# Norm sums on GpSimd, block transposes on VectorE, and column-tiled products in a four-image convolution network

## Chip, cores and metric

The kernel runs on one core of one Trainium2 chip. The metric is the device time of one execution in microseconds (us). Before the change its median over three runs is 3120.36 us (3120.36 to 3121.54).

## What is computed

Four images of 32 x 32 pixels and 16 channels go through four residual layers. Each layer adds to `x` a function of the group-normed `x` (8 groups of two channels, over all pixels of one image):

```python
x = x + conv(_gn(x), M0, W0, G0)
x = x + conv(_gn(x), M1, W1, G1)
x = x + interval(_gn(x), W0, b0, W1, b1, W2, b2)
x = x + conv(_gn(x), M3, W3, G3)
```

A convolution layer is heavy, because every one of the 1024 output pixels has a 3 x 3 kernel of its own (`G`), which is slid over the whole image:

```python
first   = einsum('ijyx,byxc->bijc', M, inputs)
shifted = conv(inputs, kern)          # 1024 x 16 filters, 3 x 3 x 16
diff    = relu(inputs - shifted)
second  = einsum('ijyx,bijyxc->bijc', W, diff)
return first - second
```

The interval layer pools over intervals (running maximum and minimum of a 32 x 32 triangle) and then does two steps of a dynamic program, with `sigmoid(f @ Wf + r @ Wr + b)` and a maximum over the split point, and a last product with `W2`. `f` is 33 x 33 x 32 for the first step; in the second step, and in the last product, the 16 hidden channels of the step before are put in front of it.

## The kernel before

The four images are two groups of two (`NG`, `GB`). A group's activations are one tile `X[g]`: 128 partitions are 128 pixels, and the free axis holds eight pixel blocks (`NT`) of two images by 16 channels (`GC` = 32). Six phases follow each other, (layer, group) in the order L59 (`phases`) gives; the interval layer is no phase of its own but is done ahead of the last convolution of each group.

**The convolution loop** (`conv_layer`, L457) has 8 pixel blocks x 16 filters x 2 images = 256 tiles in a phase, 1536 in all. A tile is six matmuls (L484): three slots of 64 rows, each as two row halves that run side by side, into a pair of PSUM banks. Slots 0 and 1 are fp32, for which the trace has two records to a matmul, slot 2 is fp32r with one record, so a tile has ten PE records. Then one VectorE instruction (L494) takes the minimum with zero, multiplies by the row of `W` and sums. There are three such bank pairs (`psum`, L55 and L58), and two more single banks (`bank`, L61) for everything else.

**Weights** come in units of eight filters, 16 tiles each: 1.5 MB `raw` by DMA from the SyncE queue, four buffers deep; `prep` (L134) subtracts a mask on GpSimd and starts the third slot on ScalarE, `prep_rest` (L149) finishes it on VectorE.

**The order of the work** is written out by hand, and each engine takes its instructions in program order. What must happen for the next phase is a generator, `behind` (L510). The loop asks it for its next piece after a tile; `yield n` puts the next piece n tiles later (L503 to L505). The pieces for the next phase are `interval_layer` (only ahead of the last convolution layer), `before_conv` and `first_term`. The first `before_conv` runs ahead of the loop, with nothing to hide it (L530 to L537).

**Pieces that matter here.** `group_norm` (L162) sums over the free axis on VectorE (L167), sums over the partitions with a matmul by a matrix of constants (L174), subtracts the mean (L184), does the same with the squares, takes the root on ScalarE (L192) and scales (L195). `before_conv` (L200) then transposes the result with TensorE (L209), copies it from PSUM on ScalarE (L215), writes it to a padded image `xs` in DRAM (L221) and reads it back as shifted copies `im` (L234). `interval_layer` (L325) puts the normed values and their negatives through TensorE transposes (L341), pools with VectorE maxima (L361, L366), and has two steps with GpSimd additions (L417) and VectorE maxima (L424). The left-hand products of a step are in `left` (L379): the output has 128 partitions, four quarters of the rows of `f` by 32 channels. Each quarter is one matmul over the full 128 output columns with a weight that is zero outside its 32 columns, so that four matmuls add up to the tile:

```python
for q in range(NQ):
    nc.tensor.matmul(
        o, lhsT=wf[q], rhs=r[:, QI * q : QI * (q + 1), :],
        start=hidden is None and q == 0, stop=q == NQ - 1,
    )
```

Steps after the first have one more matmul ahead, of the hidden channels by a block-diagonal 128 x 128 weight (L384).

Of the kernel before, what the change touches and what calls it, by code (L numbers as in the profile page):

```python
# [1 line left out]

# [5 lines left out]

F32 = mybir.dt.float32
F32R = mybir.dt.float32r  # L10
AF = mybir.ActivationFunctionType
ALU = mybir.AluOpType
AX = mybir.AxisListType

P = 128
B, H, C = 4, 32, 16
NG = 2
GB = B // NG
GC = GB * C
NL = 3  # L20
NP = H * H
NT = NP // P
HP = H + 2
NPP = HP * HP
HI = H // 2
PITCH = HI * HP
RUN = (HI - 1) * HP + H
ROWS = P // H
# [4 lines left out]
NQ = 4  # L33
QI = H // NQ
# [3 lines left out]
def net_kernel(ctx: ExitStack, tc: tile.TileContext, x, convs, iv_w, iv_b, out):  # L38
# [9 lines left out]
    nc = tc.nc  # L48
    ctx.enter_context(tc.manual_schedule())

    const = ctx.enter_context(tc.tile_pool(name="const", bufs=1))
    wpool = ctx.enter_context(tc.tile_pool(name="wpool", bufs=2))
    work = ctx.enter_context(tc.tile_pool(name="work", bufs=1))
# [7 lines left out]
    def bank(name):  # L61
        return psum.tile([P, 512], F32, tag="one", bufs=2, name=name)
# [24 lines left out]
    load_chunk(0)  # L87


    mean_w = const.tile([P, P], F32, name="mean_w")  # L90
    nc.vector.memset(mean_w, 1.0 / (2 * NP))
    eps = const.tile([P, 1], F32, name="eps")
    nc.vector.memset(eps, 1e-5)
    ident = const.tile([P, P], F32, name="ident")
# [22 lines left out]

    xs = [dram.tile([GC, NPP], F32, name=f"xs{g}") for g in range(NG)]
    zero = const.tile([P, HP], F32, name="zero")
    xt = [const.tile([P, 2, ROWS, HP], F32, name=f"xt{g}") for g in range(NG)]  # L120
    im = [const.tile([P, 3, GB, PITCH], F32, name=f"im{g}") for g in range(NG)]
    im9 = [const.tile([P, GB, PITCH], F32R, name=f"im9{g}") for g in range(NG)]

# [35 lines left out]
    def pair_view(ap):  # L159
        return ap.rearrange("p t (g s) -> p t g s", s=2)  # L160

    def group_norm(g, name, dst):  # L162


        def sums(src, name):
            part = work.tile([P, GC // 2], F32, tag="part", name=f"part_{name}")
            nc.vector.tensor_reduce(  # L167
                part, src.rearrange("p t (g s) -> p g t s", s=2), axis=AX.XY, op=ALU.add
            )
            return part  # L170

        def mean_of(part, name):
            ps = bank(f"ps_{name}")
            nc.tensor.matmul(ps[:, : GC // 2], lhsT=mean_w, rhs=part, start=True, stop=True)  # L174
            return ps[:, : GC // 2]

        part = sums(X[g], f"m{name}")
        yield 2
        m = mean_of(part, f"m{name}")
        yield 1  # L180
        mean = work.tile([P, GC // 2], F32, tag="mean", name=f"mean_{name}")
        nc.vector.tensor_copy(mean, m)
        xc = work.tile([P, NT, GC], F32, tag="xc", name=f"xc_{name}")
        nc.vector.tensor_tensor(pair_view(xc), pair_view(X[g]), spread(mean), ALU.subtract)  # L184
        yield 1
        sq = work.tile([P, NT, GC], F32, tag="sq", name=f"sq_{name}")
        nc.vector.tensor_tensor(sq, xc, xc, ALU.mult)
        part = sums(sq, f"v{name}")
        yield 2
        v = mean_of(part, f"v{name}")  # L190
        rstd = work.tile([P, GC // 2], F32, tag="rstd", name=f"rstd_{name}")
        nc.scalar.activation(rstd, v, AF.Sqrt, bias=eps)  # L192
        yield 2
        nc.vector.reciprocal(rstd, rstd)
        nc.vector.tensor_tensor(pair_view(dst), pair_view(xc), spread(rstd), ALU.mult)  # L195
        yield 2

    xns = {}

    def before_conv(g, layer):  # L200
        xn = work.tile([P, NT, GC], F32, tag="xn", bufs=2, name=f"xn_{g}_{layer}")
        xns[g] = xn
        yield from group_norm(g, f"c{g}{layer}", xn)

        ps = bank(f"ps_t{g}{layer}")
        for m in range(2):
            nc.tensor.transpose(  # L209
                ps[:, m * P : (m + 1) * P],  # L210
                xn[:, 4 * m : 4 * m + 4, :].rearrange("p t m -> p (t m)"),
                ident,
            )
        yield 1
        nc.scalar.copy(  # L215
            xt[g][:, :, :, 1 : 1 + H],
            ps[:, : 2 * P].rearrange("p (m r x) -> p m r x", m=2, x=H),
        )
        inner = xs[g][:, HP : HP + H * HP].rearrange("p (m t n) -> p t m n", m=2, t=4)
        for t in range(4):  # L220
            (nc.scalar if t % 2 else nc.sync).dma_start(  # L221
                inner[:, t],
                xt[g][GC * t : GC * (t + 1)].rearrange("p m r x -> p m (r x)"),
            )
        yield 2
        xsv = xs[g].rearrange("(b c) n -> c b n", b=GB)
        at = 0
        for slot, row, tap in [(2, row, 8) for row in range(4)] + [
            (tap // 4, tap % 4, tap) for tap in range(8)
        ]:  # L230
            for h in range(2):
                off = (HI * h + tap // 3) * HP + tap % 3
                r0 = 64 * h + C * row
                (nc.scalar, nc.sync)[at % 2].dma_start(  # L234
                    im[g][r0 : r0 + C, slot, :, :RUN], xsv[:, :, off : off + RUN]
                )
                at += 1
        yield 9
        halve(im9[g], im[g][:, 2], low_x)
        yield 2  # L240
        halve_rest(im9[g], im[g][:, 2], low_x)
# [37 lines left out]
    def constants():  # L279
        nc.vector.tensor_reduce(  # L280
            stack, ident.rearrange("p (j m) -> p m j", m=GC), axis=AX.X, op=ALU.add
        )
        nc.scalar.dma_start(wv, iv_w)
        nc.scalar.dma_start(bv, iv_b)
        mask8 = const.tile([P, 8], F32, name="mask8")
        nc.vector.tensor_reduce(
            mask8, ident.rearrange("p (k c) -> p k c", c=C), axis=AX.X, op=ALU.add
        )
        mask2 = const.tile([P, GB], F32, name="mask2")
        nc.vector.tensor_reduce(  # L290
            mask2, ident.rearrange("p (s b c) -> p b s c", b=GB, c=C), axis=AX.XY, op=ALU.add
        )
        yield 2

        def blocks(dst, k, mask, n):
            p = dst.shape[0]
            nc.gpsimd.tensor_tensor(
                dst,
                wv[:p, k, :].unsqueeze(1).to_broadcast([p, n, C]),
                mask[:p].unsqueeze(2).to_broadcast([p, n, C]),  # L300
                ALU.mult,
            )

        for k, name in ((0, "f0"), (3, "f1"), (6, "f2")):

            t = const.tile([64, (2 * NQ - 1) * GB, C], F32, name=name)
            nc.gpsimd.memset(t, 0.0)
            at = (NQ - 1) * GB
            blocks(t[:, at : at + GB, :], k, mask2, GB)
            t = t.rearrange("p k c -> p (k c)")  # L310
            iv[name] = [t[:, GC * (NQ - 1 - q) : GC * (NQ - 1 - q) + P] for q in range(NQ)]
            yield 1
        for k, name in ((1, "r0"), (4, "r1")):
            t = const.tile([64, NQ * GB, C], F32, name=name)
            for q in range(NQ):
                blocks(t[:, q * GB : (q + 1) * GB, :], k, mask2, GB)
            iv[name] = t.rearrange("p k c -> p (k c)")
            yield 1
        for k, name in ((2, "h1"), (5, "h2")):
            t = const.tile([P, 8, C], F32, name=name)  # L320
            blocks(t, k, mask8, 8)
            iv[name] = t.rearrange("p k c -> p (k c)")
            yield 1

    def interval_layer(g):  # L325

        R = 2 * GC
        xn2 = ivp.tile([P, NT, 2, GC], F32, tag="xn2", name=f"xn2_{g}")
        yield from group_norm(g, f"i{g}", xn2[:, :, 0, :])
        nc.gpsimd.tensor_scalar_mul(xn2[:, :, 1, :], xn2[:, :, 0, :], -1.0)  # L330

        M = H // 2
        pp = [ivp.tile([R, H + M, M + H], F32, tag=f"pp{k}", name=f"pp{k}_{g}") for k in range(2)]
# [1 line left out]
            nc.gpsimd.memset(t, -BIG)  # L335
        yield 3
        raw = pp[1][:, :H, M:]
        for half in range(2):
            ps = bank(f"ps_iv{g}{half}")
            for t in range(4):  # L340
                nc.tensor.transpose(  # L341
                    ps[:R, t * P : (t + 1) * P],
                    xn2[:, 4 * half + t].rearrange("p s m -> p (s m)"),
                    ident,
                )
            yield 1
            nc.scalar.copy(
                raw[:, HI * half : HI * (half + 1), :],
                ps[:R].rearrange("p (i j) -> p i j", j=H),
            )  # L350
        upper = [[-1, H], [1, H]]
        nc.gpsimd.affine_select(
            out=pp[0][:, :H, M:], in_=raw, pattern=upper, compare_op=ALU.is_ge, fill=-BIG,
# [25 lines left out]
        def left(name, wf, hidden=None, wh=None):  # L379

            ps = bank(f"ps_{name}{g}")
            o = ps[:, : QI * T1]
            if hidden is not None:
                nc.tensor.matmul(o, lhsT=wh, rhs=hidden, start=True, stop=False)  # L384
            for q in range(NQ):
                nc.tensor.matmul(  # L386
                    o, lhsT=wf[q], rhs=r[:, QI * q : QI * (q + 1), :],
                    start=hidden is None and q == 0, stop=q == NQ - 1,
                )
            return o.rearrange("p (i k) -> p i k", k=T1)  # L390

# [135 lines left out]
        if phase == len(phases) - 1:  # L527
            nc.sync.dma_start(out[1 - g], X[1 - g])

    start = before_conv(*phases[0])  # L530
    next(start)
    v = ident.rearrange("p (h q c) -> p q c h", h=2, q=4)
    nc.vector.tensor_reduce(pick, v[:, 0], axis=AX.X, op=ALU.add)
# [72 lines left out]
```

## Time and profile before

| Figure | Value |
|---|---|
| Span of the profiled execution | 3119.8 us |
| VectorE busy | 2100.3 us, 67% |
| ScalarE busy | 147.2 us, 5% |
| GpSimd busy | 289.2 us, 9% |
| Convolution matmuls, slots 0 and 1 (L484) | 12288 records, 2920.4 us |
| VectorE reduction of a tile (L494) | 1536 of 1224 ns |
| Norm sums by matmul (L174) | 4 groups of records, 6.8 us busy together |
| Transposes ahead of a convolution (L209) | 12 of 324 ns |
| Transposes of the interval layer (L341) | 16 of 279 ns |
| Left products (L386 and L384) | 48 records of 391 ns and 8 of 438 ns |
| Granted TensorE clock | 1.000 |

Busy time of a matmul record says little alone, since records overlap: the convolution's two row halves run side by side. The chain of work that ended last, in order of time, is the view to read: it follows the span back from its last instruction, and each piece begins where the one before it ends. A piece `PE pc L484 x40` is a run of 40 convolution records, that is four tiles.

### The profile page before, as it was taken

How to read it: one execution, taken by the hardware profiler on the slowest of the kernel's cores; microseconds unless marked ns; L12 is line 12 of the kernel's file. 1: busy time of each engine (PE TensorE's matmuls, PEld its weight loads, DVE VectorE, ACT ScalarE, POOL GpSimd, SP SyncE). 2: the span in 40 equal slices, each digit the busy share in tenths (PEclk: the TensorE clock that was granted, in tenths of full speed). 3: DMA queues.
4: the chain of work that ended last, by engine and by line, in shares of the span. 5: the costliest groups of instructions: out<-in, count | busy, mean ns of one | idle time of the engine just before them, and what ended most of it. 6: DMA issues, size and time to landing. Idle time of an engine off the chain costs nothing.

```text
span 3119.8 us, 37923 instructions
## 1 busy us (share of the span) xinstructions
PE 3089.7 (99%) x15792; PEld 1568.0 (50%) x15792; DVE 2100.3 (67%) x3348; ACT 147.2 (5%) x159; POOL 289.2 (9%) x173
## 2 busy tenths in 40 slices
PE   6999999999999999999999999999999999999999
PEld 4444455444444444444446654444664444444444
DVE  4656666666666666666677766667776666666666
ACT  0000000000000000000000000000100000000000
POOL 2000000000000000000013300002230000000000
PEclk9999999999999999999999999999999999999999
DMA  4322111321111231211111132121113211111100
GB/s 144 123 102 75 48 68 48 125 75 66 50 62 60 69 124 48 75 48 68 48 70 52 48 118 75 48 75 48 68 48 103 97 48 70 48 72 51 67 28 2
DMA packets 32462, 215.21 MB, mean 69 GB/s; under 512 B 5665, under 2 KB 7713, under 8 KB 18465
## 3 DMA queue, kind: packets, MB, share of 16 engines
q1 hardware_dynamic: 27168, 207.02, 18.4%
q10 hardware_dynamic: 4992, 5.74, 0.9%
q8 instruction: 124, 2.03, 0.3%
q14 instruction: 50, 0.40, 0.0%
q0 software_dynamic: 128, 0.02, 0.0%
HBM read 211.64 MB, written 1.12 MB: 68 GB/s over the span
## 4 chain that ended last, share of the span: by engine, by line
PE 99%; DMA 1%; DVE 0%; ACTq 0%; issue 0%; ACT 0%
PE pc L484 97%; PE pf L255 1%; PE pfs L263 0%; DMA im<-xs 0%; PE ps_l L386 0%; DMA X<-in_x 0%; PE ps_r L397 0%; PE ps_l L384 0%; PE ps_t L209 0%; PE ps_vc L174 0%; PE ps_iv L341 0%; DMA xs<-xt 0%; PE ps_mc L174 0%; DVE xc_c L184 0%; ACTq L234 0%; DVE junk L494 0%
## 5 line engine op out<-in xcount | busy, mean ns | idle before, releaser
L484 PE MATMUL pc<-im,raw 64*128 64x512 f32 x12288 | 2920.4, 590 | 13.2 <-DMA im<-xs 13.2
L494 DVE SCALAR_TENSOR_TENSOR junk<-pc,WT 128x1024 f32<-128x1024 f32 x1536 | 1880.0, 1224 | 990.4 <-PE pc L484 986.6
L484 PEld LDWEIGHTS pc<-im,raw 64*128 64x128 f32 x12288 | 1237.2, 186 | 1137.5 <-issue 746.6
L484 PE MATMUL pc<-im,W 64*128 64x512 f32 x3072 | 1293.2, 803 | 0.0
L484 PEld LDWEIGHTS pc<-im,W 64*128 64x128 f32 x3072 | 321.1, 186 | 355.6 <-issue 343.5
L140 POOL TENSOR_TENSOR raw<-raw,pick 128x1024 f32<-128x1024 f32 x96 | 182.0, 1898 | 2278.5 <-DMA raw<-in_g 2216.9
L111 ACT ACTIVATE W<-raw,low_w 128x1024 fp32r<-128x1024 f32 x96 | 110.3, 1149 | 2198.0 <-PE pc L484 2170.1
L494 DVE DVE_READ_ACCUMULATOR junk<-pc,WT 128x1 f32 x1536 | 127.6, 83 | 0.0
L114 DVE SCALAR_TENSOR_TENSOR W<-raw,low_w,W 128x1024 fp32r<-128x1024 f32 x96 | 122.9, 1280 | 0.0
L417 POOL TENSOR_TENSOR dp_b<-ft_b,rt_r 128x1089 f32<-128x1089 f32 x16 | 39.1, 2449 | 101.6 <-ACT ft_b L410 51.5
L417 POOL TENSOR_TENSOR dp_a<-ft_a,rt_r 128x1089 f32<-128x1089 f32 x16 | 37.2, 2327 | 79.9 <-DVE s_a L424 50.2
L255 PE MATMUL pf<-MT,xn 128*32 128x512 f32 x192 | 23.1, 598 | 0.0
L424 DVE TENSOR_REDUCE s_b<-dp_b 128x33 f32<-128x1089 f32 x16 | 20.5, 1283 | 0.0
L424 DVE TENSOR_REDUCE s_a<-dp_a 128x33 f32<-128x1089 f32 x16 | 20.5, 1282 | 0.0
L114 DVE SCALAR_TENSOR_TENSOR im<-im,low_x,im 128x1088 fp32r<-128x1088 f32 x6 | 9.1, 1523 | 14.6 <-DMA im<-xs 14.6
L259 ACT COPY fs<-pf 128x512 f32<-128x512 f32 x12 | 7.0, 586 | 240.1 <-PE pf L255 240.1
L330 POOL TENSOR_SCALAR xn<-xn 128x256 f32<-128x256 f32 x2 | 1.7, 856 | 151.0 <-DVE xn L195 151.0
L506 DVE TENSOR_TENSOR X<-X,acc 128x32 f32<-128x32 f32 x48 | 13.6, 283 | 1.6
L263 PEld LDWEIGHTS pfs<-stack,fs 128*128 128x128 f32 x96 | 11.2, 191 | 3.4 <-issue 3.4
L361 DVE TENSOR_TENSOR pp<-pp 64x1024 f32<-64x1024 f32 x10 | 12.1, 1213 | 0.0
L366 DVE TENSOR_TENSOR pp<-pp 64x1024 f32<-64x1024 f32 x10 | 12.1, 1213 | 0.0
L255 PEld LDWEIGHTS pf<-MT,xn 128*32 128x32 f32 x192 | 5.0, 109 | 14.1 <-issue 14.1
(81 smaller groups left out, 160.1 us busy)
## 6 DMA issues: line engine op xcount, KB each, us to landing
raw<-in_g SPq DMA_DIRECT2D x96, 1536.0 KB, 6.6
WT<-in_w SPq DMA_DIRECT2D x48, 512.0 KB, 6.3
MT<-in_mt SPq DMA_DIRECT2D x12, 2048.0 KB, 8.3
im<-xs SPq DMA_DIRECT2D x72, 67.8 KB, 3.2
im<-xs ACTq DMA_DIRECT2D x72, 67.8 KB, 3.3
xs<-xt SPq DMA_DIRECT2D x12, 34.0 KB, 1.7
xs<-xt ACTq DMA_DIRECT2D x12, 34.0 KB, 1.8
X<-in_x ACTq DMA_DIRECT2D x2, 128.0 KB, 5.1
```

Source lines behind the costliest of these rows:

```text
L111: nc.scalar.activation(dst, src, AF.Copy, scale=mask[:, 1:2])
L114: nc.vector.scalar_tensor_tensor(dst, src, mask[:, 0:1], dst.bitcast(F32), op0=ALU.mult, op1=ALU.add)
L140: nc.gpsimd.tensor_tensor(raw[:, 1], raw[:, 1], pick[:, f0 : f0 + FU].unsqueeze(2).to_broadcast([P, FU, P]), ALU.subtract,)
L255: nc.tensor.matmul(ps[32 * j : 32 * j + 32, :], lhsT=xn[:, pt, :], rhs=mt[:, pt, :], start=pt < 4, stop=pt >= 4, tile_position=(0, 32 * j),)
L263: nc.tensor.matmul(ps[:, GC * t : GC * (t + 1)], lhsT=fs[:, t // 4, t % 4 * P : (t % 4 + 1) * P], rhs=stack, start=True, stop=True,)
L361: nc.vector.tensor_tensor(pp[k][:, :H, M:], a[:, :H, M:], a[:, s : H + s, M:], ALU.max)
L366: nc.vector.tensor_tensor(pp[k][:, :H, M:], a[:, :H, M:], a[:, :H, M - s : M - s + H], ALU.max)
L417: nc.gpsimd.tensor_tensor(t, ft[:, i, :].unsqueeze(1).to_broadcast([P, T1, T1]), rt, ALU.add,)
L424: nc.vector.tensor_reduce(s[:, i - 1, :], last, axis=AX.X, op=ALU.max)
L484: nc.tensor.matmul(ps[:, h, :], lhsT=w[:, f % FU, :], rhs=v[:, :, :H], start=slot == 0, stop=slot == 2,)
L494: nc.vector.scalar_tensor_tensor(junk, ps.rearrange("p h n -> p (h n)"), 0.0, chunks[n], op0=ALU.min, op1=ALU.mult, accum_out=acc[:, t, co ...
L506: nc.vector.tensor_tensor(X[g][:, t], X[g][:, t], acc[:, t], ALU.add)
```

## The change

It takes work off TensorE.

- **Norm sums.** The sum over partitions becomes GpSimd's `partition_all_reduce` on the 128 x 16 partial sums. The division by the number of elements moves into the multiplication that copies the mean, and into the scale of the root. The waits are rewritten: five tiles lie between the sum and its use instead of one for the mean, and five more for the variance. The first norm, ahead of the loop, keeps the matmul (`on_pe=True`).
- **Transposes.** VectorE's `transpose`, which transposes blocks of 32 x 32, replaces TensorE's transposes and the copies from PSUM. Ahead of a convolution it is one instruction over 128 x 256; in the interval layer it is four over 32 x 256, and the negatives are then made by one ScalarE multiplication. As the layout of a block transpose differs, the store to `xs` is in runs of one image row (34 numbers) instead of four rows.
- **Left products.** A quarter has a 32-column weight and writes only its own 32 output partitions; the hidden product is four 32 x 32 products on the diagonal in place of one of 128 x 128.
- The constants shrink with it (`f0` to `f2`, `h1`, `h2`, no `mask8`).

```diff
         def mean_of(part, name):
+            if not on_pe:
+                m = work.tile([P, GC // 2], F32, tag="sum", name=f"sum_{name}")
+                nc.gpsimd.partition_all_reduce(m, part, channels=P, reduce_op=bass_isa.ReduceOp.add)
+                return m
             ps = bank(f"ps_{name}")
-            nc.tensor.matmul(ps[:, : GC // 2], lhsT=mean_w, rhs=part, start=True, stop=True)
+            nc.tensor.matmul(ps[:, : GC // 2], lhsT=ones, rhs=part, start=True, stop=True)
             return ps[:, : GC // 2]
 
         part = sums(X[g], f"m{name}")
         yield 2
         m = mean_of(part, f"m{name}")
-        yield 1
+        yield 5
         mean = work.tile([P, GC // 2], F32, tag="mean", name=f"mean_{name}")
-        nc.vector.tensor_copy(mean, m)
+        nc.vector.tensor_scalar_mul(mean, m, 1.0 / (2 * NP))
...
         v = mean_of(part, f"v{name}")
+        yield 5
         rstd = work.tile([P, GC // 2], F32, tag="rstd", name=f"rstd_{name}")
-        nc.scalar.activation(rstd, v, AF.Sqrt, bias=eps)
+        nc.scalar.activation(rstd, v, AF.Sqrt, bias=eps, scale=1.0 / (2 * NP))
...
-        ps = bank(f"ps_t{g}{layer}")
-        for m in range(2):
-            nc.tensor.transpose(
-                ps[:, m * P : (m + 1) * P],
-                xn[:, 4 * m : 4 * m + 4, :].rearrange("p t m -> p (t m)"),
-                ident,
-            )
-        yield 1
-        nc.scalar.copy(
-            xt[g][:, :, :, 1 : 1 + H],
-            ps[:, : 2 * P].rearrange("p (m r x) -> p m r x", m=2, x=H),
-        )
-        inner = xs[g][:, HP : HP + H * HP].rearrange("p (m t n) -> p t m n", m=2, t=4)
-        for t in range(4):
-            (nc.scalar if t % 2 else nc.sync).dma_start(
-                inner[:, t],
-                xt[g][GC * t : GC * (t + 1)].rearrange("p m r x -> p m (r x)"),
-            )
+        nc.vector.transpose(
+            xt[g][:, :, 1 : 1 + H], xn
+        )
+        inner = xs[g][:, HP : HP + H * HP].rearrange("p (t r n) -> p r t n", r=ROWS, n=HP)
+        for r in range(ROWS):
+            (nc.scalar if r % 2 else nc.sync).dma_start(inner[:, r], xt[g][GC * r : GC * (r + 1)])
...
-        for half in range(2):
-            ps = bank(f"ps_iv{g}{half}")
-            for t in range(4):
-                nc.tensor.transpose(
-                    ps[:R, t * P : (t + 1) * P],
-                    xn2[:, 4 * half + t].rearrange("p s m -> p (s m)"),
-                    ident,
-                )
-            yield 1
-            nc.scalar.copy(
-                raw[:, HI * half : HI * (half + 1), :],
-                ps[:R].rearrange("p (i j) -> p i j", j=H),
+        for row in range(ROWS):
+            nc.vector.transpose(
+                raw[:GC].rearrange("p (t r) j -> p r t j", r=ROWS)[:, row], xi[H * row : H * (row + 1)]
             )
+        yield 1
+        nc.scalar.mul(raw[GC:], raw[:GC], -1.0)
...
+            quarters = [slice(GC * q, GC * (q + 1)) for q in range(NQ)]
             if hidden is not None:
-                nc.tensor.matmul(o, lhsT=wh, rhs=hidden, start=True, stop=False)
-            for q in range(NQ):
+                for s in quarters:
+                    nc.tensor.matmul(o[s], lhsT=wh[s], rhs=hidden[s], start=True, stop=False)
+            for q, s in enumerate(quarters):
                 nc.tensor.matmul(
-                    o, lhsT=wf[q], rhs=r[:, QI * q : QI * (q + 1), :],
-                    start=hidden is None and q == 0, stop=q == NQ - 1,
+                    o[s], lhsT=wf, rhs=r[:, QI * q : QI * (q + 1), :],
+                    start=hidden is None, stop=True,
                 )
...
-    start = before_conv(*phases[0])
+    start = before_conv(*phases[0], on_pe=True)
```

## The prediction

> **What bounds the kernel now.** I read the page's busy shares first, then its chain of work that ended last, then stretches of that chain in order of time.
>
> ```profile
> PE 3089.7 (99%) x15792; PEld 1568.0 (50%) x15792; DVE 2100.3 (67%) x3348; ACT 147.2 (5%) x159; POOL 289.2 (9%) x173
> PE 99%; DMA 1%; DVE 0%; ACTq 0%; issue 0%; ACT 0%
> ```
>
> TensorE is 99% of the chain: from the first convolution tile on nothing else ends last. So whatever is taken out of its stream shortens the kernel, and work on other engines costs nothing until it stops that stream. What does one small matmul cost there? The chain from 540 to 660 us (start, length, what), around the norm and transpose for one convolution:
>
> ```profile
> 553.49 0.33 PE ps_mc L174 x2
> 553.81 8.05 PE pc L484 x40
> 561.86 0.32 PE ps_vc L174 x2
> 562.18 8.04 PE pc L484 x40
> 570.23 0.37 PE ps_t L209 x2
> 570.60 51.16 PE pc L484 x256
> 621.75 1.85 PE pf L255 x16
> ```
>
> Runs of 4 and of 26 tiles (x256 has four records missing) took 8.04 and 51.16 us: (51.16 - 8.04) / 22 = 1.960 us a tile. From the mean's matmul to the variance's are 8.37 us, four tiles are 7.84, so one norm sum costs 0.53 us, not its 0.33: the run behind it loses 0.20 as the array empties and refills. The variance's costs 0.53 too; the transposes cost 570.23 to 621.75 less 26 tiles, 51.52 - 50.96 = 0.56. The interval layer of the second group, in the same view:
>
> ```profile
> 2118.68 0.56 PE ps_iv L341 x4
> 2119.24 2.16 PE pc L484 x9
> 2121.40 0.56 PE ps_iv L341 x4
> ...
> 2188.66 1.56 PE ps_l L386 x7
> 2190.22 62.94 PE pc L484 x320
> ...
> 2260.87 0.64 PE ps_l L384 x2
> 2261.51 1.75 PE ps_l L386 x7
> ```
>
> A half of its transposes costs 2.72 - 1.96 = 0.76. The first left product costs 1.56 + 0.20 = 1.76; one with hidden channels 0.64 + 1.75 + 0.20 = 2.59.
>
> Is VectorE near the limit? A tile takes 1224 + 83 ns of 1.960 us, 0.65 us is free. There are three bank pairs, so I estimate that it may run 2 x 1.96 - 1.27 = 2.65 us late before TensorE waits. Where two extra operations meet (timeline of VectorE):
>
> ```profile
> 1617.59 1.21 DVE L361 TENSOR_TENSOR pp<-pp 64x1024 f32<-64x1024 f32 x1
> 1618.73 1.27 DVE L114 SCALAR_TENSOR_TENSOR W<-raw,low_w,W 128x1024 fp32r<-128x1024 f32 x1
> 1619.92 1.21 DVE L494 SCALAR_TENSOR_TENSOR junk<-pc,WT 128x1024 f32<-128x1024 f32 x1
> ```
>
> The tile's reduction before began at 1616.44, so this one is 1.5 us late, yet the chain there is one run of 30 tiles in 59.00 us, 30 x 1.960 + 0.20.
>
> **What the Trainium skill says.** "TensorE: Matmul & The Clock Gate", Part 3 (Packing small matmuls): tiles in different column groups run at once, for little more than the time of one. The trace agrees: `pf` is 8 matmuls of 512 columns on four column tiles (L255), 16 records; in sequence they would need 16 x 0.43 = 6.8 us (the first left product, 8 passes of 264 columns in 1.76, gives 0.22 a pass, and so 0.43 for 512), and they cost 1.85 + 0.20 = 2.05. "TensorEngine Tiling (Array Packing)", Key Properties: changing the tiling mode drains the array; its Gotcha 1 says that different row tiles cannot use one PSUM bank at the same time. The drain is seen: `ps_l` without hidden channels, on 64 rows as the convolution, costs what its passes cost, while the 128-row hidden matmul adds 0.83 for two passes, 0.44, so about 0.39 for a mode and back; `pf` gives 2.05 - 4 x 0.43 = 0.33. The bank rule no trace here shows. "GPSIMD Engine Reference", section 3.2, has a partition-axis reduction of 128 x 2048 at 247.7 us; section 2.1 puts a first call to a freshly loaded kernel near 6 us. No run here shows either.
>
> **The change, part by part.**
>
> *Norm sums.* On PE, two leave each of five convolution norms and two interval norms (the first norm keeps its matmuls): 14 x 0.53 = -7.4 us. GpSimd gets 14 reductions of 16 columns. The skill's rate gives 247.7 / 2048 x 16 = 1.9 us; with 6 for a load, about 8 (estimates). Low bound: one small GpSimd operation, 0.23 us (L297). High bound: I allow 20. I take 2 to 8. The wait this adds: VectorE's multiplication for the mean stands 2 + 5 tiles, 13.7 us, behind the partial sum, and behind it queue the tile reductions, for whose bank pairs TensorE waits. The variance has 9 tiles, 17.6 us, to VectorE's reciprocal, with ScalarE's root between, behind which only weight preparation queues. So up to 13 us cost nothing. On GpSimd, mask subtractions queue behind the sum, but they run about two units ahead (2216.9 us of its idling is for a unit's DMA), and before, it sat 75.6 us for the interval norm (L330) without TensorE noticing. Cost 0.
>
> *Transposes.* On PE -5 x 0.56 - 4 x 0.76 = -5.8 us. VectorE gets five of 128 x 256 and eight of 32 x 256. "VectorE: DVE Perf Modes", The three transpose paths, has 128 x 128 at 311 ns in bf16; the nearest row here is a multiplication of 128 x 256, 0.42 us (L187). I take 0.42; upper bound twice that. Interval: four in one go, 1.7 us (3.4 at most), within 2.65 as priced, over it by under 1 us twice at the bound. Cost 0. The ScalarE negation replaces two copies of 0.58, hidden in four tiles.
>
> *Left products.* The first: two rounds of four tiles, 2 x 0.22 + 0.33 for the mode = 0.77, saves 1.0, twice: -2.0. With hidden channels, if the four diagonal tiles overlap: 4 x 0.22 for both products, and three mode changes at about 0.18, 0.55: 1.43, saves 1.16, four times: -4.6. If the one shared bank makes the diagonal tiles wait for each other, 8 passes in place of 2 add 1.3 each: +5.3 in all.
>
> *Start.* Ahead of the loop nothing hides. Out go transposes and copy, 13.56 to 14.86 in the chain, 1.30 us; in comes one transpose with its handover, 0.5: -0.8. The store to `xs` has 1024 pieces of 136 B for 256 of 544 B. Its stretch was 2.10 us; pieces of 544 B took 32 ns. At 32 again, 64 a DMA engine instead of 16, it grows by 48 x 0.032 = 1.5; at 17 (what the 4-byte ones beside them take) by 0.6; at three times 32, as "DMA: Bandwidth & Descriptors" (table at its head) warns of read-modify-write under 512 B, by 5.6. I take +1.2: net +0.4. Later stores lie under nine tiles of waiting: cost 0. The longer waits make the interval phase some 191 of 256 tiles long, so nothing runs over its end.
>
> Sum: -7.4 - 5.8 - 2.0 - 4.6 + 0.4 = -19.4; 3120.4 - 19.4 = 3101.
>
> **Rivals.**
> A, all hides and the tiles overlap: 3101. Chance 0.62.
> B, the diagonal tiles run one after another, or modes cost double: 3101 + 5.3 = 3106. For: the bank rule. Against: `pf` overlaps in one bank, though with one row group. 0.16.
> C, the pieces of 136 B cost 96 ns at the start, and the block transposes take twice as long and stop TensorE: 3101 + 4.4 + 2 = 3107. 0.10.
> D, slower: GpSimd's sum is the new bound. At 20 us it is 6.3 beyond the mean's 13.7, of which 2.65 are absorbed: 3.7 x 7 = 26 us; the variance exceeds its 17.6 by 2.4, absorbed: 3101 + 26 = 3127. At 25 us: 8.7 + 4.8 = 13.5 x 7 = 94, 3195. For: GpSimd operations are the slowest here (2449 ns at L417), and nothing shows this one. Against: 16 columns are little. 0.08.
> E, a sum of 17 to 20 us eats the gain, or other stops do: 3114 to 3126. 0.04.
>
> **How the numbers follow.** A's time is predicted. The range takes A to C with their unknowns: 3097 (store without growth, cheaper modes) to 3112; D, E and 0.05 of tails lie outside. Faster by over 0.2% means under 3114.1: A, B, C, 0.88. Same is E, 0.04, slower D, 0.08.
>
> **What would show it.** In the chain after, `ps_mc`, `ps_vc`, `ps_t`, `ps_iv` are gone after the first tile, and convolution runs pass there at 1.960 a tile. `ps_l` pieces with 0.20 added give 0.77 and 1.43; 2.7 with hidden channels is B. GpSimd's sum under 13 us, and VectorE's wait for it zero; a wait of VectorE for it, followed by TensorE waiting for `junk`, is D. First steady tile at 29.89 + 0.4. Wrong it would be by a sum over 13.7 us, or by transposes near 1 us each.

## The result, and the profile after

The changed kernel takes 3103.43 us (median of six runs, 3102.53 to 3106.23), the kernel before 3120.57 (3119.03 to 3121.54). The ratio is 0.9947, 95% interval 0.9934 to 0.9960: 17 us faster, where 19.4 were forecast. In the pair of profiled executions the span falls from 3119.8 to 3100.8 us.

The page's busy shares and the engines of the chain that ended last, after the change:

```profile
PE 3069.8 (99%) x15760; PEld 1506.1 (49%) x15760; DVE 2114.4 (68%) x3361; ACT 145.7 (5%) x151; POOL 294.3 (9%) x182
PE 99%; DMA 1%; DVE 0%; issue 0%; ACTq 0%; ACT 0%; DVEq 0%
```

TensorE is the bound as before. The stretch of the chain that answers to the norm and transpose of one convolution (start, length, what; the view begins at 480 us, in the midst of a run):

```profile
479.65 151.71 PE pc L463 x774
631.36 1.85 PE pf L248 x16
```

Where the kernel before had three interruptions ahead of the first term, there is one run of convolution tiles. And the left products of the second group's interval layer, in the same view:

```profile
2189.68 0.58 PE ps_l L365 x8
2190.26 62.97 PE pc L463 x320
...
2260.93 0.58 PE ps_l L363 x8
2261.51 0.58 PE ps_l L365 x8
```

A run of tiles takes 0.20 us beyond its tiles, called refilling below. With it, the first product costs 0.78 us (1.76 before), one with hidden channels 1.36 (2.59 before). GpSimd's timeline around an interval norm, with the idle time ahead of an operation and its releaser in brackets:

```profile
1563.59 0.45 POOL L175 PARTITION_ALL_REDUCE sum_mi<-part_mi  x1 [58.19 <-DVE part_mi L167]
1580.70 0.44 POOL L175 PARTITION_ALL_REDUCE sum_vi<-part_vi  x1 [16.67 <-DVE part_vi L167]
1588.59 1.89 POOL L140 TENSOR_TENSOR raw<-raw,pick 128x1024 f32<-128x1024 f32 x1 [7.44 <-issue]
```

A sum takes 0.45 us and starts when VectorE hands it the partial sums. The next weight preparation comes 7.44 us behind the sum, in which GpSimd waited for nothing that the profile shows. Such a pause of 7.1 to 7.5 us lies between a sum and the next weight preparation throughout. The expectations below call it a load; the profile gives it no name.

Two things are there that the forecast did not have. One is a stop of TensorE at the first group's interval layer. Timeline of VectorE around it:

```profile
1606.19 1.77 DVE L323 STREAM_TRANSPOSE pp<-xi 32x256 f32<-32x256 f32 x4
...
1609.14 4.27 DVE L114 SCALAR_TENSOR_TENSOR W<-raw,low_w,W 128x1024 fp32r<-128x1024 f32 x1
```

And of GpSimd:

```profile
1609.19 1.27 POOL L329 TENSOR_SCALAR_AFFINE_SELECT pp<-pp 64x1024 f32<-64x1024 f32 x1 [14.80 <-ACT pp L327]
1610.44 1.89 POOL L140 TENSOR_TENSOR raw<-raw,pick 128x1024 f32<-128x1024 f32 x1
```

VectorE's weight operation (L114) takes 4.27 us instead of 1.28, while two GpSimd operations run; it ends 1.08 us behind the second of them. It stands behind the burst of four transposes, so the reductions are late, and TensorE waits: from 1177.16 us the chain takes 488.72 us for 248 tiles, and in the second profile of the same kernel, without the stop, 486.69. So one tile takes 2.03 us more than the others.

The other is in the tile itself. A long uninterrupted run in the chain after, and one before:

```profile
668.75 471.00 PE pc L463 x2400
```

```profile
1168.72 403.96 PE pc L484 x2055
```

240 tiles in 471.00 - 0.20 us are 1.9617 us each. The 206 tiles before (some records are missing) took 403.96 - 0.20, 1.9600 each. Over 1535 tiles 0.0017 us are 2.6 us, more than the forecast's step for the first left products (2.0).

The start of the loop also differs from execution to execution: VectorE's first reduction began at 32.62 us in the profile before, at 30.49 in the one after, and at 33.52 in a second profile of the changed kernel (e0_after below). The second reduction came 3.13, 1.97 and 3.77 us behind the first, where a tile is 1.96. So the profile after had a start 3.3 us shorter than the one before, by chance, and the 19.0 us between the two spans agree with the forecast's 19.4 better than they should. Differences of some 3 us between single profiles are not read as effects here; medians over runs and lengths of pieces are.

### The profile page after: what moved, and what is told of

It reads as the page before. It is cut to its first block, busy times and chain, and to the rows that moved or that the text cites. A ratio compares the mean times of both kernels' runs of the same rounds, so it can differ in the third digit from the quotient of the medians.

```text
span 3100.8 us, 37902 instructions
## 1 busy us (share of the span) xinstructions
PE 3069.8 (99%) x15760; PEld 1506.1 (49%) x15760; DVE 2114.4 (68%) x3361; ACT 145.7 (5%) x151; POOL 294.3 (9%) x182
## 4 chain that ended last, share of the span: by engine, by line
PE 99%; DMA 1%; DVE 0%; issue 0%; ACTq 0%; ACT 0%; DVEq 0%
PE pc L463 97%; PE pf L248 1%; PE pfs L256 0%; DMA im<-xs 0%; DMA X<-in_x 0%; DVE junk L473 0%; PE ps_r L376 0%; PE ps_l L365 0%; DMA xs<-xt 0%; PE ps_l L363 0%; DVE xc_c L188 0%; DVE pp L323 0%; PE ps_y L427 0%; PE ps_vc L178 0%; DVE xt L212 0%
## 5 line engine op out<-in xcount | busy, mean ns | idle before, releaser
L473 DVE SCALAR_TENSOR_TENSOR junk<-pc,WT 128x1024 f32<-128x1024 f32 x1536 | 1879.7, 1224 | 958.5 <-PE pc L463 953.2
L463 PEld LDWEIGHTS pc<-im,raw 64*128 64x128 f32 x12288 | 1187.5, 186 | 1185.1 <-issue 800.5
L463 PE MATMUL pc<-im,W 64*128 64x512 f32 x3072 | 1251.1, 804 | 0.0
L463 PEld LDWEIGHTS pc<-im,W 64*128 64x128 f32 x3072 | 298.7, 186 | 365.8 <-issue 364.8
L114 DVE SCALAR_TENSOR_TENSOR W<-raw,low_w,W 128x1024 fp32r<-128x1024 f32 x96 | 134.6, 1402 | 0.0
L114 DVE SCALAR_TENSOR_TENSOR im<-im,low_x,im 128x1088 fp32r<-128x1088 f32 x6 | 8.1, 1347 | 13.3 <-DMA im<-xs 13.3
```

Of the source, the lines that this page charges most:

```text
L114: nc.vector.scalar_tensor_tensor(dst, src, mask[:, 0:1], dst.bitcast(F32), op0=ALU.mult, op1=ALU.add)
L463: nc.tensor.matmul(ps[:, h, :], lhsT=w[:, f % FU, :], rhs=v[:, :, :H], start=slot == 0, stop=slot == 2,)
L473: nc.vector.scalar_tensor_tensor(junk, ps.rearrange("p h n -> p (h n)"), 0.0, chunks[n], op0=ALU.min, op1=ALU.mult, accum_out=acc[:, t, co ...
```

## The experiments

**The three parts alone.** Theory: a matmul taken out of the stream is worth its piece in the chain and the 0.2 us of refilling, and the other engines hide what they get. Rival: what GpSimd does about its sums, or VectorE's bursts, disturbs the loop and gives some of it back. Each part of the diff was put into the kernel before by itself. The norm sums:

```diff
+            if not on_pe:
...
+                nc.gpsimd.partition_all_reduce(m, part, channels=P, reduce_op=bass_isa.ReduceOp.add)
...
-            nc.tensor.matmul(ps[:, : GC // 2], lhsT=mean_w, rhs=part, start=True, stop=True)
...
-        yield 1
+        yield 5
```

> Only the norm sums move to GpSimd, with their new waits; transposes and left products stay as before. Price theory (each matmul taken out of the stream is worth its piece plus 0.2 us of refilling, and nothing else changes): 14 x 0.525 = 7.4 us less than before, so near 3113; no wait of TensorE for VectorE; first tile as before, near 29.9 us. Rival (the [...]7.2 to 7.5 us that GpSimd pays after a sum, and the sums themselves, disturb the loop): the steady tile grows from 1.960 to about 1.962 us here and not in the other two parts, which gives back some 2.6 us, so near 3116.

3112.78 us against 3119.88, ratio 0.9976 (0.9967 to 0.9985): 7.1 us, as the pieces say (7.4). A run of 217 tiles in the chain:

```profile
1182.67 425.52 PE pc L489 x2170
```

(425.52 - 0.20) / 217 = 1.9600. GpSimd's sums and pauses do not touch the tile. The transposes:

```diff
-            nc.tensor.transpose(
-                ps[:, m * P : (m + 1) * P],
...
+        nc.vector.transpose(
+            xt[g][:, :, 1 : 1 + H], xn
+        )
```

> Only the transposes move to VectorE, with the store in runs of one image row; sums and left products as before. Price theory: 5 x 0.57 + 4 x 0.755 = 5.9 us less, and if the start of the changed kernel came from this part, 2 us more, so near 3112.5: the reads of the padded image at the start take 88 ns a piece as in the changed kernel, not 215. Rival (the shorter start was chance): the reads take 215 ns again, the start is 0.4 us longer than before, and the time is near 3115. If a burst of four transposes on VectorE stops TensorE by itself, each of the two bursts costs up to 2 us more.

3115.08 us, ratio 0.9984 (0.9977 to 0.9990): 4.8 us, 3.1 to 7.2 by the interval. The pieces are 5.9; the start takes something back. The store to the padded image, in the chain of this kernel:

```profile
14.58 3.45 DMA xs<-xt
```

It ends at 18.03 us, where before it was 15.25 + 2.10 = 17.35: +0.7. The reads behind it took 186 ns a piece of 2168 bytes (median), and in the changed kernel's second profile 216, so the 88 ns of its first profile were chance. There was no stop at either burst of transposes here. The left products:

```diff
-            t = const.tile([64, (2 * NQ - 1) * GB, C], F32, name=name)
...
+            t = const.tile([64, GB, C], F32, name=name)
...
+                for s in quarters:
+                    nc.tensor.matmul(o[s], lhsT=wh[s], rhs=hidden[s], start=True, stop=False)
-            for q in range(NQ):
+            for q, s in enumerate(quarters):
```

> Only the left products go on 32-column tiles. Price theory: the first product falls from 1.78 to 0.78 us and those with hidden channels from 2.615 to 1.353, 2 x 1.0 + 4 x 1.26 = 7.1 us less, so near 3113.5; the steady tile stays at 1.960. Rival (changes of tiling mode or smaller weights change the loop's own rate): the steady tile differs from 1.960 here.

3115.09 us, ratio 0.9985 (0.9978 to 0.9991): 4.8 us and not 7.1, although the products cost what was expected (0.58 us a piece). The tile is why; a run of 206 tiles:

```profile
1169.15 404.30 PE pc L478 x2060
```

(404.30 - 0.20) / 206 = 1.9617: the rival's answer, and in this part alone. And the whole change again, on the same chip as its parts:

> The changed kernel again, on the chip of its parts. If the parts add up: 3120.5 less the three gains. If the steady tile of 1.962 us was chance of chip or run, it is 1.960 here; if it belongs to the program, 1.962 again. The stop of 2.0 us near 1613 us [...]may come or not.

3105.84 us, ratio 0.9956 (0.9942 to 0.9969). The three gains add to 16.7, measured are 14.0 here and 17.1 in the first comparison. The interval here reaches from 9.7 to 18.1 us, so the parts may simply add up; no loss from their meeting is shown. The tile is 1.9617 us again (240 tiles in 471.00), so it belongs to the program. The stop near 1613 us did not come: there VectorE's weight operation took 1.28 us.

**What slows the tile.** The run just quoted ends at 1573 us, and the first left product in that trace is at 1666, so the products themselves do not slow it. But this part also shrinks the constants (`f0` to `f2`, `h1`, `h2`, `mask8`) by 3104 bytes a partition, and the weight buffers lie behind them: `raw` begins at byte 59200 of a partition instead of 62304. An unused constant moves them by 32:

```diff
+        pad = const.tile([P, 8], F32, name="pad")
+        nc.gpsimd.memset(pad, 0.0)
         mask2 = const.tile([P, GB], F32, name="mask2")
```

> The changed kernel with one unused constant of 32 bytes a partition ahead of the buffers that follow the constants, so that the weights lie at 59232 instead of 59200 in a partition; nothing else differs. Address theory (the smaller constants moved the weights from an address that is 32 past a multiple of 64 to a multiple of 64, and this slows every tile by 0.0017 us): the steady tile is 1.960 us again and the time 2.6 us under the changed kernel's. Rival (the column-tiled products themselves, or the shift of some 3 KB, slow the loop): 1.9617 us stays.

> The kernel before with the same unused 32 bytes: the weights move from 62304 to 62336, a multiple of 64. Address theory: the steady tile grows to about 1.9617 us and the time by 2.6 us, near 3122.5. Rival: 1.960 us and 3120 stay.

The changed kernel with the pad: 3101.57 us, ratio 0.9943 (0.9930 to 0.9955). The kernel before with it: 3124.57 us, ratio 1.0015 (1.0008 to 1.0021). One long run of the first and one of the second:

```profile
669.92 470.60 PE pc L465 x2396
```

```profile
1169.05 404.64 PE pc L486 x1864
```

240 tiles (four records missing) in 470.40 are 1.9600 us, 206 tiles in 404.44 are 1.9633. So 32 bytes that nobody reads bring the changed kernel's tile back, and cost the kernel before 4.9 us. (In time alone the pad's gain for the changed kernel is not clear of the noise, since the two intervals overlap; the length of its tile is.) It is the address of what lies behind the constants: the granted clock reads 1.00 in all these runs of tiles, and VectorE's reduction takes 1224 ns on average in every one of the kernels. By the remainder of `raw`'s address on division by 128, the tile took:

| Remainder | Kernels | us a tile |
|---|---|---|
| 96 | before, e1_norms, e2_transposes, f1_after_pad, and the padded h1 and i1 below | 1.9600 |
| 64 | the changed kernel (two profiles), e3_left, g1 below | 1.9617 |
| 0 | f2_before_pad | 1.9633 |
| 32 | j1 and j2 below | 1.960 to 1.967, changing from phase to phase |

j1 and j2 differ in their late sums too, so the last row is no test of the address alone. The images `im`, TensorE's other operand, lie ahead of the constants and stay where they are, but other buffers moved with `raw`. Which of them counts, and whether 128 is the period, stays open.

**Are the long waits needed?** The sums are ready 0.45 us behind the partial sums. The waits were set back:

```diff
         m = mean_of(part, f"m{name}")
-        yield 5
+        yield 1
...
         v = mean_of(part, f"v{name}")
-        yield 5
```

> The changed kernel with the waits of the kernel before: one tile instead of five ahead of the mean's use, none instead of five ahead of the root. If a sum takes the 0.45 us that the record shows[...], VectorE never waits for it and the time is that of the changed kernel within 1 us. Rival (a load of 7.2 to 7.9 us lies between partial sum and sum): where one does, VectorE waits 2 to 4 us for it, and TensorE stops up to 2 us at each, up to some 15 us in all.

3102.41 us (3100.88 to 3102.84), ratio 0.9943 (0.9931 to 0.9956). No time is lost. Timeline of GpSimd at a norm of the first phase, and then of VectorE:

```profile
54.04 0.45 POOL L175 PARTITION_ALL_REDUCE sum_mc<-part_mc  x1 [14.64 <-DVE part_mc L167]
```

```profile
59.38 0.17 DVE L186 TENSOR_SCALAR mean_c<-sum_mc 128x16 f32<-128x16 f32 x1
```

The sum is there at 54.49 and used at 59.38. GpSimd had been idle for 14.64 us when the partial sum came, since its weight preparation runs units ahead, so a pause on the way into the sum is hidden in that time; the one behind the sum keeps nobody waiting.

**The stop behind the burst.** Is it the burst of 1.77 us, or the meeting of VectorE's two-input operation with GpSimd's? The weight operation was moved by two tiles, the burst left alone, in the padded kernel:

```diff
-                if f % FU == 4:
+                if f % FU == 5:
                     prep_rest(u + 1)
```

> The padded changed kernel with the weights' second half (the two-input VectorE operation of 1.28 us) two tiles later in each unit; the interval layer's four transposes stay in one burst. Port theory (the stop of 2.04 us needs that VectorE operation to meet a GpSimd operation, which holds it up to 4.27 us, right behind the burst): no stop at either burst, and a time 0 to 4 us under the padded kernel's 3101.6, depending on how many of its runs were hit. Rival (the burst of 1.77 us alone stops TensorE): a stop of some 2 us stays at one or both bursts.

3099.80 us (3099.47 to 3101.97), ratio 0.9938 (0.9925 to 0.9950). VectorE's timeline at the first burst:

```profile
1606.71 1.77 DVE L325 STREAM_TRANSPOSE pp<-xi 32x256 f32<-32x256 f32 x4
...
1612.59 1.35 DVE L114 SCALAR_TENSOR_TENSOR W<-raw,low_w,W 128x1024 fp32r<-128x1024 f32 x1
```

The burst is as long as before, the weight operation short again, and no tile at either burst is longer than the others. The padded kernel f1_after_pad, which differs in this alone, had a stop of 2.0 us at both bursts in its profile, with L114 at 4.27 us each time. One profile without stops would be weak, since the stop comes and goes, but all profiles agree: of the twelve bursts in after, e0_after, e2_transposes, f1, g1 and i1, the three with L114 at 4.27 us behind them have the stop, the nine others, with 1.35 at most, have none. So the burst alone does no harm; with a weight operation held behind it, it does. In the profile after, weight operations of 3.31 and 3.37 us away from a burst (at 1674.79 and 2190.87) stop nothing; whether 4.27 alone would was not tried. It is a near tie: at the second group's burst, L114 began at 2127.26 and GpSimd's selection at 2127.31, the same 0.05 us apart as at the first, and there VectorE took 1.28 us and the selection 2.37 instead of 1.27. The Trainium skill ("GPSIMD Engine Reference", section 1, Specifications) says that GpSimd's memory interfaces are shared with VectorE and contended by VectorE instructions with two SBUF inputs. The traces agree: L114 reads two SBUF tiles; the tile reduction, which reads PSUM and one SBUF tile, took 1223 ns on average in the 220 cases where a GpSimd two-input operation overlapped it, and 1224 over all.

**What late sums would cost.** The forecast's slower case was never tried by the change itself. A detour makes each sum late without changing its value:

```diff
-                return m
...
+                nc.gpsimd.tensor_tensor(share, m, per_p, ALU.mult)
...
+                nc.gpsimd.partition_all_reduce(again, share, channels=P, reduce_op=bass_isa.ReduceOp.add)
+                return again
```

In j1_late_sums the waits stay long; j2_late_sums_short has those of g1_short_waits as well.

> The padded changed kernel with GpSimd's sums made late on purpose: behind each sum a two-input operation and a second sum,[...] so that the result comes some 16 us behind the partial sum instead of 0.45. The result is the same number. The waits stay at five tiles. By the working of the prediction's slower case, the mean is due after 13.3 us, so VectorE gets it 2.7 us late, of which 2.65 are absorbed, and the variance is due after 17 us: no more than 1 us lost in all, near 3101. Rival (nothing is absorbed): 7 x 2.7 = 19 us lost.

> The same late sums with the waits of the kernel before (one tile ahead of the mean's use, none ahead of the root). The mean is due after 5.5 us and comes 10.5 late, of which 2.65 are absorbed: 7.9 lost; the variance is due after 7.1 us and comes 8.9 late: 6.3 lost; seven norms lose 7 x 14.2 = 99 us, near 3200, and TensorE waits for VectorE's reduction there. If GpSimd hides the loads in another way, the loss is smaller than half of that.

With the long waits 3127.78 us, ratio 1.0028 (1.0018 to 1.0039), where no more than 1 us was expected to be lost: 26 us over the padded kernel. GpSimd's timeline at a norm of the second phase:

```profile
567.92 0.21 POOL L177 TENSOR_TENSOR share_mc<-sum_mc,per_p 128x16 f32<-128x16 f32 x1 [7.46 <-issue]
574.12 0.44 POOL L179 PARTITION_ALL_REDUCE again_mc<-share_mc  x1 [5.99 <-issue]
```

VectorE's there, and at the variance in the first phase:

```profile
98.82 0.25 DVE L203 RECIPROCAL rstd_c<-rstd_c 128x16 f32<-128x16 f32 x1 [12.54 <-ACT rstd_c L201]
...
574.59 0.17 DVE L190 TENSOR_SCALAR mean_c<-again_mc 128x16 f32<-128x16 f32 x1 [1.33 <-POOL again_mc L179]
```

The pauses of 7.46 and 5.99 us come wherever GpSimd goes from a sum to a two-input operation or back, 5.7 to 8.6 us each in j1 and j2. At the second phase's mean VectorE waits 1.33 us and no tile grows: lateness within the slack is absorbed, as worked out. But at 90.9 us one tile takes 11.9 us more: TensorE stands for 9.84 us, and the next 3.67 us it runs at a granted clock of 0.50. There, in the first phase, a weight preparation stood between the two sums and brought two further pauses, so that the variance's sum began 12 us late. At the two interval layers the late sums delay GpSimd's fill of `pp`, the transposes wait for that (2.2 us at the first), and then meet the weight operation: stops of 4.3 and 5.2 us. The tile, at yet another address (remainder 32 in the table), is 1.960 to 1.967 us from phase to phase, 5.6 us in all. 11.9 + 4.3 + 5.2 + 5.6 = 27, against a padded execution without stops.

With short waits 3219.60 us, ratio 1.0319 (1.0305 to 1.0333). Its waits (who, for whom, us in total, times, longest):

```profile
PE pc L470 <- DVE junk L480: 82.5, 14, 8.9
...
DVE mean_c L190 <- POOL again_mc L179: 49.9, 5, 11.7
```

118 us over the padded kernel, 99 were expected. VectorE waits for the sum and TensorE for VectorE, 14 times, 82.5 us together: 8.9 us at the first mean, 6.1 to 7.4 at the others, and 4.4 to 5.3 at a variance, where 7.9 and 6.3 were worked out. The sums were not as late as that working took them to be: the second phase's mean came 14.4 us behind its partial sum (565.86 to 580.26) and not 16, and 14.4 - 5.5 - 2.65 = 6.2 fits the stop of 6.08 us there. The rest was in no forecast. The two stretches behind that stop (length, busy time and instructions of PE, PEld, DVE, ACT and POOL, then the granted clock):

```profile
582.13:586.70 4.57, 4.57 (x12) 2.20 (x14) 3.39 (x7) 0.00 (x0) 0.44 (x1) 0.50 0.00 0
586.70:594.40 7.70, 7.70 (x40) 3.41 (x36) 3.26 (x5) 0.00 (x0) 0.21 (x1) 1.00 0.01 2
```

TensorE starts again at a granted clock of 0.50, with 12 records in 4.57 us, and goes on at 1.00, with 40 in 7.70. The same comes behind each of the 14 stops. Those stretches are 62.6 us long, and half of that, 31 us, is what they cost (an estimate); 82.5 + 31 is 114 of the 118. Behind the stop of 1.77 us in the profile after, the clock stays at 1.00.

**More of the same.** Since VectorE's block transposes are free, the first term can use them. Each 32-column tile computes, for all eight pixel blocks, the 32 pixels that will lie on its own 32 partitions, so a block transpose yields the layout of `X`, and the eight transposing matmuls (`pfs`) go. The interval layer's rows are dealt to the quarters in turn for the same reason. The file also has the pad and one tile between the second and the third transpose of a burst:

```diff
-                nc.tensor.matmul(
-                    ps[32 * j : 32 * j + 32, :], lhsT=xn[:, pt, :], rhs=mt[:, pt, :],
-                    start=pt < 4, stop=pt >= 4, tile_position=(0, 32 * j),
-                )
...
+                rows = mt[:, q, :].rearrange("p (t j x) -> p j t x", t=NT, j=4)
+                for j in range(4):
+                    nc.tensor.matmul(
+                        ps[32 * j : 32 * j + 32, : NT * GC], lhsT=xn[:, pt, :], rhs=rows[:, j],
+                        start=pt == 0, stop=pt == NT - 1, tile_position=(0, 32 * j),
+                    )
+        nc.vector.transpose(fs, ps[:, : NT * GC].rearrange("p (t x) -> p t x", t=NT))
...
-                    o[s], lhsT=wf, rhs=r[:, QI * q : QI * (q + 1), :],
+                    o[s], lhsT=wf, rhs=r[:, q : H : NQ, :],
```

> Built on the padded changed kernel. The first term is computed with a column tile for each quarter of a pixel block, over 256 columns, so that VectorE's block transpose gives the layout of X and the eight matmuls that transposed it (2.1 us a layer) go away; the final transposes of the interval layer go to VectorE too, with rows dealt to the quarters in turn; and one tile lies between the second and the third block transpose of the interval layer. Price theory: a layer's first term falls from 2 x 2.054 + 2.10 = 6.21 us to 16 rounds of 0.213 and two mode changes of 0.35, 4.1, six times: 12.6 us; the final transposes 1.1 us; the pad 2.6 us: 16.3 us under the changed kernel. Rival (64 short matmuls on column tiles are bound by their issue, not by their columns): the two pieces cost 3 us or more each and most of the 12.6 us is lost.

3086.63 us (3083.57 to 3087.45), ratio 0.9892 (0.9878 to 0.9905): 33 us under the kernel before and 17 to 19 under the changed one, where 16.3 were expected. The first term in its chain:

```profile
629.88 1.86 PE pf L249 x32
631.75 23.72 PE pc L455 x120
655.47 1.86 PE pf L249 x32
```

Each half costs 1.86 + 0.20 as before, with twice the records of half the columns, and nothing follows them. Issue does not bind at 256 columns.

## Why the prediction was right, step by step

- **What bounds**: right. 99% of the chain is TensorE in both kernels, and the parts gave what their pieces said, once the tile is counted.
- **Norm sums, -7.4**: right; alone they gave 7.1. GpSimd's cost was put at 2 to 8 us a sum from a rate of the Trainium skill ("GPSIMD Engine Reference", section 3.2); it is 0.45, with a pause of 5.7 to 8.6 us beside it, which comes at every change between sums and two-input operations and not once. Cost 0 was right, and the new waits were not even needed (g1_short_waits).
- **Transposes, -5.8 and 0 on VectorE**: the pieces are right (5.9), and so is 0.42 us an operation (0.44 measured). "Within 2.65 as priced" held for the burst, which alone stops nothing (i1_no_meeting), but not for what can stand behind it: a two-input operation held by GpSimd, 2.04 us at a burst in some executions.
- **Left products, -6.6**: the diagonal tiles overlap, in one bank, so rival B's bank rule (the Trainium skill, "TensorEngine Tiling (Array Packing)", Gotcha 1) did not bind here: eight hidden records cost 0.58 us, no more than the eight of the second product. A product with hidden channels came to 1.36 and not 1.43. On the pieces alone the gain is 2 x 0.98 + 4 x 1.23 = 6.9.
- **Start, +0.4**: the number fits, the working does not. The store ended 0.5 us later than before in the profile after and 0.7 in e2_transposes, and its stretch grew by 1.24 in the profile after where 1.2 was taken. But the pieces of 136 bytes took 13 to 14 ns each, so by the forecast's own sum (64 of them for 16 of 32 ns) they add 0.35 us. What fills the rest is open, and the agreement is luck. Rival C's 96 ns a piece is refuted.
- **The term that was missing**: the forecast took the tile at 1.960 us for both. The smaller constants, listed in the change, moved the weight buffers, and the tile grew by 0.0017 us, 2.6 us in all. The forecast was 19.4 us less, 17.1 were measured, and 2.6 is the size of that miss; with the pad the time is 3101.57. The agreement in the last microsecond is not to be trusted, since a stop of 2 us comes or does not. In the pair of profiles the account closes: -7.4 - 5.9 - 6.9 for the pieces, -3.3 for the chance start, +2.6 for the tile and +2.0 for one stop are -18.9, and the spans differ by 19.0.
- **D, the slower case**: the wait it works out for one late sum is right where it could be seen: absorbed up to the slack (1.33 us in j1_late_sums), then lost (6.2 worked out with the lateness as it was, 6.08 measured in j2_late_sums_short). It left out two things. Late sums also push GpSimd's other work (j1), and behind a long stop TensorE runs at a granted clock of 0.50, 31 us in j2. The 99 us expected there for 118 measured are nearer than the working deserves: the waits were over-estimated and the clock was missing.

## What to carry to other kernels

Where one engine is the whole chain, price an operation on it as the difference between starts, refilling included, not by its own length; here that was 0.53 us for a matmul of 16 columns. When a diff changes the size of any tile, look at what lies behind it in memory, and compare the inner loop's period before and after to the nanosecond. On engines with slack, a burst is judged with the longest thing that can stand behind it, and a two-input VectorE operation beside GpSimd work can take three times its time (1.28 us became 4.27). And a stop of the bound engine is not priced by its length alone: look at the granted clock behind it.

## What was not expected of the hardware

- Where the buffers behind the constants lie changes the period of the same ten matmul records: 1.9600, 1.9617 or 1.9633 us, by 32-byte steps of all of them.
- GpSimd's sum over 128 partitions of 16 columns takes 0.44 to 0.45 us (1.36 once in g1 and once in j2), and 5.7 to 8.6 us pass, under no instruction's name, when GpSimd goes from it to a two-input operation or back. The Trainium skill ("GPSIMD Engine Reference", section 2.1) has about 6 us for the first call to a freshly loaded kernel; that this is it was not shown.
- VectorE and GpSimd hold each other for about whole instructions: 1.28 us became 4.27, or GpSimd's 1.27 became 2.37. Which of them waits the recorded starts do not tell here, since VectorE's was 0.05 us ahead in both cases.
- Behind stops of 4.4 us and more TensorE's granted clock read 0.50 for some microseconds after it started again (j2_late_sums_short, all 14 stops); behind stops of 1.77 us (after) and 3.10 us (j1_late_sums) it stayed at 1.00.
- Four 32 x 32 tiles on the diagonal, writing one bank, run at once: 0.58 us for eight records of 264 columns.
